# A wider row pitch for the two large tiles of the last layers, and message products taken by column

## The chip, the cores and the metric

The kernel runs on one core of a Trainium2 chip. The metric is the device time of one execution in microseconds. Five engines work side by side, each in the order of its own queue: PE (matrix products), DVE and ACT (elementwise work), POOL (elementwise work as well) and SP, which here only issues DMAs.

## What is computed

The input x is 4 images of 128 x 128 pixels with 128 channels. Four layers follow, each of the form x + f(group norm of x): a deformable convolution, a convolution that runs along the rows of the image as a recurrence, a message layer and a triangle product. The change concerns the last two; cut to what matters:

```python
# layer 2, messages: inputs = group norm of x, [b, m, k, d]
message_m = sum(inputs, axis=2)            # over k
message_k = sum(inputs, axis=1)            # over m
z = inputs @ Wself.T + (message_m @ Wm.T)[:, :, None] + (message_k @ Wk.T)[:, None]
x = x + z
# layer 3, triangle: xn = layer_norm(group norm of x)
left  = (xn @ left_w  + left_b)  * sigmoid(xn @ lgate_w + lgate_b)
right = (xn @ right_w + right_b) * sigmoid(xn @ rgate_w + rgate_b)
out   = einsum('bkjd,bkid->bijd', left, right)
out   = layer_norm(out) * sigmoid(xn @ ogate_w + ogate_b)
x = x + out @ to_out_w + to_out_b
```

## The kernel before

The first two layers, `deform_layer` and `scan_layer`, take the first 3,950 us or so and leave their result in device memory as x2T, channels first. `message_and_triangle` does the rest, one image after the other, in three parts.

`taken_in(b)` forms the tile X of one image: 128 channels on the partitions and, in each, 128 x 128 values of 4 bytes, with the image's column w (named j later on) ahead of its row h (named i), so that one column is a run of 512 B. Its first loop, the message loop, takes eight image rows at a time (16 iterations an image): SP loads them as x2c (L1274), POOL adds the two message terms into zc (L1276), PE multiplies x2c by the weights in two products of 512 columns each (L1282), and DVE adds product and zc into X (L1285). Because the product has its columns in the order (h, w) and X lies in the order (w, h), the store of L1285 steps by 512 B from element to element. Two `bn_stats` on DVE follow (L1290), which read X in runs of four elements. After the loop eight DMAs store X to device memory as x3T (L1295), to be added to the output later. The second loop takes 16 columns at a time: PE multiplies X by a centring matrix (L1316), ACT squares the result (L1322) and writes it back into X (L1325), the deviations go to device memory, are inverted and come back spread over all partitions as rwide (L1350), and DVE multiplies X by them (L1354).

`multiplied(b)` forms the tile T: PE multiplies X by the stacked weights (L1369), ACT takes the sigmoid (L1374), DVE multiplies the two and stores them into T by channel (L1375), each channel being a row of 128 values, 512 B; then products of two such rows (L1393) go back into T through ACT (L1397). The gate goes to device memory (L1382 to L1389).

`given_out(b, T)` goes through the result by column j. It reads `prod[:, :, j]`, 128 elements of one j, one from each row of T and so 512 B apart: once for the statistics (L1409, DVE, 16 at a time), once for the normalized u (three of four on ACT, L1438, the fourth on POOL, L1434). Then PE transposes u (L1451), ACT scales (L1453), POOL multiplies by the gate that was loaded (L1446, L1454), PE adds x3 and multiplies by the output weights (L1457, L1460), ACT copies to the gate's tile (L1461), and SP stores that (L1462).

The order of work: the queues are in the order of the program, up to small moves by the scheduler. While `given_out(b)` runs, every half step of it (four columns j) is followed by two steps of the generator `taken_in(b + 1)`, so the message loop of the next image lies beside the output of this one. The tile pools set how far things run ahead: zc and sq share one buffer (the tag in_work), x2c has two buffers, rwide two of its own, the gate two, X and T one each. All DMAs of this stage are issued from SP's queue.

Of the kernel before, what the change touches and what calls it, by code (L numbers as in the profile page):

```python
# [10 lines left out]
F32 = mybir.dt.float32  # L11
I32 = mybir.dt.int32
BF16 = mybir.dt.bfloat16
AF = mybir.ActivationFunctionType
ALU = mybir.AluOpType
# [4 lines left out]
P = 128  # L20
B = 4
S = 128
# [10 lines left out]
NQ = 4  # L33
DQ = P // NQ
# [1120 lines left out]
def message_and_triangle(tc, c, x2T, counted, w2, w3, out, x3T, gateT, stdT):  # L1155
# [4 lines left out]
    nc = tc.nc  # L1160
# [4 lines left out]
    JB = 8  # L1165
    with ExitStack() as ctx:
# [29 lines left out]
        with tc.tile_pool(name="l3prep", bufs=1) as prep, tc.tile_pool(  # L1196
            name="l3ps_w", bufs=2, space=PSUM
# [48 lines left out]
        xs = {}  # L1246

        def taken_in(b):

            X = xs[b] = big.tile([P, S, S], F32, name="X")  # L1250
# [21 lines left out]
            for y0 in range(0, S, JB):  # L1272
                x2c = two.tile([P, JB, S], F32, name="x2c")
                nc.sync.dma_start(x2c, x2T[b, :, y0 : y0 + JB, :])  # L1274
                zc = one.tile([P, JB, S], F32, name="zc", tag="in_work")
                nc.gpsimd.tensor_tensor(  # L1276
                    zc, z[:, 0, y0 : y0 + JB].unsqueeze(2).to_broadcast([P, JB, S]),
                    z[:, 1].unsqueeze(1).to_broadcast([P, JB, S]), ALU.add,
                )
                pz = pair()  # L1280
                for h in range(2):
                    nc.tensor.matmul(  # L1282
                        pz[:, h], lhsT=ws, rhs=x2c[:, 4 * h : 4 * h + 4], start=True, stop=True
                    )
                nc.vector.tensor_tensor(  # L1285
                    X[:, :, y0 : y0 + JB].rearrange("p w h -> p h w"),
                    pz.rearrange("p n (h w) -> p (n h) w", w=S), zc, ALU.add,
                )
                for h in range(0, JB, 4):
                    nc.vector.bn_stats(  # L1290
                        stats3[:, (y0 + h) // 4, :], X[:, :, y0 + h : y0 + h + 4]
                    )
                yield
# [16 lines left out]
            for j0 in range(0, S, 2 * JB):  # L1310
                pv = single()
                for h in range(2):
                    j1 = j0 + h * JB
                    px = pair()
                    for n in range(2):
# [10 lines left out]
                        X[:, j1 : j1 + JB, :].rearrange("p j i -> p (j i)"), flat, AF.Identity,  # L1326
                        bias=ct,
# [19 lines left out]
                for h in range(4):  # L1347
                    j1 = j0 + h * 4
                    rw = two.tile([P, 4 * S], F32, name="rwide")
# [3 lines left out]
                    flat = X[:, j1 : j1 + 4, :].rearrange("p j i -> p (j i)")  # L1353
                    nc.vector.tensor_tensor(flat, flat, rw, ALU.mult)  # L1354
# [4 lines left out]
        def multiplied(b):  # L1359
# [3 lines left out]
            T = big.tile([P, NQ + 1, DQ, S], F32, name="T")  # L1363
# [186 lines left out]
```

## Time and profile before

| What | us |
|---|---|
| Median of 3 runs | 5,704.68 (5,692.88 to 5,705.37) |
| The profiled execution, its own time | 5,716.77 |
| Span of the profile | 5,715.0 |
| PE busy | 5,055.9 (88%) |
| DVE busy | 3,207.3 (56%) |
| ACT busy | 2,556.8 (45%) |
| POOL busy | 1,162.6 (20%) |
| DMA, mean rate over the span | 124 GB/s |

The durations in this document come from the profiled execution, which is 12 us above the median. A share of busy time over the whole span says little here, because the stages have different limits; the prediction reads the stage that the change touches, stretch by stretch. Three kinds of lines occur. A group or source line gives an instruction of one kernel line, how often it ran and its minimum, median and maximum in ns. A timeline line gives start and length in us, and in brackets how long the engine had stood idle and what ended that. The chain of waits follows back from the last instruction what released each step. One instruction's duration includes a latency that the next one overlaps, so the distance between two starts in a train is shorter than the duration.

### The profile page before, as it was taken

The numbers are of one execution on the slowest core, as the hardware profiler recorded it, in microseconds if no ns is written. First come the engines' busy times: TensorE is split into PE (matmuls) and PEld (weight loads), VectorE is DVE, ScalarE is ACT, GpSimd is POOL, SyncE is SP. The second block draws the span as 40 slices with busy tenths as digits, with TensorE's granted clock in tenths as the row PEclk, the third lists the DMA queues.
The fourth block names the chain that finished last, engine by engine and source line by source line (L and its number), as shares of the span: only waits on it lengthen the run. The fifth ranks groups of instructions, "written<-read, shape, count | busy, mean of one in ns | idle before, by whom it ended". The sixth has DMA issues, their size and how long they took to land. (4 is left out here: it accounts for less than half of the span.)

```text
span 5715.0 us, 163429 instructions
## 1 busy us (share of the span) xinstructions
PE 5055.9 (88%) x69432; PEld 4359.9 (76%) x69432; DVE 3207.3 (56%) x8190; ACT 2556.8 (45%) x5243; POOL 1162.6 (20%) x1013
## 2 busy tenths in 40 slices
PE   2898999999999999899998999997797887887886
PEld 1787788787887888788997999996474774774775
DVE  4666666666666666655555666666446245345350
ACT  1554454544545445445442333331445445446444
POOL 4222222201212012221000111112104204214112
PEclk9999999999999999999998999999999999999987
DMA  4776566665666756556442222222417317327324
GB/s 150 155 166 148 128 148 133 154 132 114 148 135 144 142 103 146 130 125 130 87 92 79 78 87 77 77 87 75 149 49 238 129 66 235 118 79 230 111 70 134
DMA packets 1273820, 710.73 MB, mean 124 GB/s; under 512 B 845645, under 2 KB 1112174, under 8 KB 1263862
## 3 DMA queue, kind: packets, MB, share of 16 engines
q1 hardware_dynamic: 1243538, 658.56, 46.1%
q10 hardware_dynamic: 29540, 41.60, 2.1%
q8 instruction: 549, 8.99, 0.7%
q14 instruction: 193, 1.58, 0.1%
HBM read 417.28 MB, written 282.55 MB: 122 GB/s over the span
## 5 line engine op out<-in xcount | busy, mean ns | idle before, releaser
L606 PE MATMUL conv_ps<-ring,wdef 128*128 128x192 f32 (+2 forms) x7632 | 1295.4, 319 | 5.8 <-DVE x1c L576 4.8
L514 DVE TENSOR_TENSOR m<-t_ps,tent 128x390 f32<-128x390 f32 x1548 | 806.9, 557 | 785.1 <-ACT tent L512 769.2
L606 PEld LDWEIGHTS conv_ps<-ring,wdef 128*128 128x128 f32 x7632 | 1141.5, 194 | 125.3 <-issue 64.0
L512 ACT COPY tent<-t_ps 128x390 f32<-128x390 f32 x1560 | 691.4, 487 | 652.6 <-PE t_ps L498 642.4
L498 PE MATMUL t_ps<-parts_of,spread 57*64 57x99 bf16 (+1 forms) x12384 | 741.7, 275 | 167.2 <-DVE m L514 145.0
L523 PE MATMUL v_ps<-m,pixels 60*64 60x108 f32 (+1 forms) x22704 | 813.7, 265 | 18.4 <-DVE m L514 8.8
L498 PEld LDWEIGHTS <-spread 57*64 57x64 bf16 x12480 | 577.5, 125 | 311.8 <-issue 264.5
L523 PEld LDWEIGHTS v_ps<-m,pixels 60*64 60x64 f32 x22704 | 674.0, 137 | 68.7 <-DVE m L514 23.1
L549 ACT COPY ring<-v_ps 128x432 f32<-128x432 f32 x1032 | 505.7, 525 | 445.1 <-PE v_ps L523 444.4
L420 POOL TENSOR_TENSOR off<-off,koff 72x512 f32<-72x512 f32 x128 | 162.7, 1271 | 1761.8 <-DVE off L417 1761.8
L1369 PEld LDWEIGHTS pair_ps<-wcat,X 128*128 128x128 f32 x4096 | 474.3, 192 | 52.3 <-POOL X L1356 23.2
L1369 PE MATMUL pair_ps<-wcat,X 128*128 128x128 f32 x4096 | 495.9, 279 | 19.8 <-POOL X L1356 18.2
L1375 DVE TENSOR_TENSOR T<-pair_ps,sig 128x512 f32<-128x512 f32 x256 | 266.8, 1043 | 424.1 <-ACT sig L1374 415.5
L1110 PEld LDWEIGHTS own_ps<-diff,wconv 128*128 128x128 f32 x4064 | 494.4, 191 | 13.2
L1110 PE MATMUL own_ps<-diff,wconv 128*128 128x128 f32 x4064 | 495.2, 273 | 0.0
L506 PE MATMUL t_ps<-parts_of,spread 57*64 57x130 bf16 x9288 | 454.2, 225 | 0.0
L1150 POOL TENSOR_TENSOR sum_h<-sum_h,x2c 128x512 f32<-128x512 f32 x128 | 162.5, 1269 | 1137.9 <-DVE x2c L1136 680.4
L438 DVE SCALAR_TENSOR_TENSOR parts<-off,parts 72x512 bf16<-72x512 f32 x384 | 296.1, 772 | 150.7 <-ACT parts L430 145.0
L1460 PE MATMUL one_ps<-outw,y 128*128 128x128 f32 x1024 | 247.6, 334 | 122.5 <-POOL y L1454 122.4
L1068 ACT ACTIVATE rowT<-x1T_ps,t_x,s_x 128x128 f32<-128x128 f32 x512 | 207.7, 568 | 313.2 <-PE x1T_ps L1064 313.2
L1460 PEld LDWEIGHTS one_ps<-outw,y 128*128 128x128 f32 x1024 | 195.2, 239 | 174.5 <-POOL y L1454 172.7
L506 PEld LDWEIGHTS <-spread 57*64 57x64 bf16 x9312 | 318.8, 108 | 0.1
(183 smaller groups left out, 6930.0 us busy)
## 6 DMA issues: line engine op xcount, KB each, us to landing
pixels<-tab SPq DMA_DIRECT2D x688, 123.8 KB
parts_of<-off SPq DMA_DIRECT2D x1032, 55.7 KB
off<-parts SPq DMA_DIRECT2D x64, 891.0 KB
tab<-rows SPq DMA_DIRECT2D x384, 128.0 KB
xin<-in_x_dram SPq DMA_DIRECT2D x128, 256.0 KB
x<-x1c SPq DMA_DIRECT2D x32, 1024.0 KB
x1rows<-x SPq DMA_DIRECT2D x128, 256.0 KB
x2T<-x2c ACTq DMA_DIRECT2D x128, 256.0 KB
```

The source lines that it names most:

```text
L438: nc.vector.scalar_tensor_tensor(parts[:, NSPLIT + i, h : h + RO, 2 : S + 2], off, 0.0, part, ALU.is_gt, ALU.mult,)
L498: nc.tensor.matmul(tp[h : h + HALF, 0, 0:n].rearrange("p (r c) -> p r c", c=PADW)[:, :, i:PADW:RX], lhsT=spread[0:k, kx // 2, i, h : h + H ...
L506: nc.tensor.matmul(tp[h : h + HALF, 1, i * PADW : (i + 1) * PADW], lhsT=spread[HALF : HALF + k, kx // 2, first + i, h : h + HALF], rhs=src ...
L512: nc.scalar.copy(tent[:, 0:n], tp[:, 0, 0:n])
L514: nc.vector.tensor_tensor(m, *pair, ALU.mult)
L523: nc.tensor.matmul(to[p1 : p1 + HALF], lhsT=pix[p0 : p0 + LANES, xb, :], rhs=m[p0 : p0 + LANES, :, RX * xb : RX * xb + w], start=True, sto ...
L549: nc.scalar.copy(to, bodies[side])
L606: nc.tensor.matmul(pc[:, at : at + rows, x0:x1], lhsT=wdef[:, side, k, :], rhs=v[:, :, k if v.shape[2] == NK else kx, x0 + kx : x1 + kx], ...
L1110: nc.tensor.matmul(own[:, n], lhsT=wt[:, 2 * j + n, :], rhs=diffs[h][:, n, :, j : j + V], start=False, stop=(n == 1 and j == NJ - 1),)
L1369: nc.tensor.matmul(pj[:, j], lhsT=X[:, j0 + j, :], rhs=wcat[:, q * 4 * DQ : (q + 1) * 4 * DQ], start=True, stop=True,)
L1375: nc.vector.tensor_tensor(T[:, q : NQ + 1 : NQ - q, :, j0 : j0 + JB], pj[:, :, 0 : 2 * DQ].rearrange("p j (n d) -> p n d j", n=2), sig.rea ...
L1460: nc.tensor.matmul(po[:, j], lhsT=y[:, j], rhs=outw, start=False, stop=True)
```

## The change

Both large tiles get rows of 132 elements (528 B) of which 128 are used. The message loop forms its product by column: the moving operand of the two products reads x2c with the row h as the inner dimension (eight elements, 512 B apart, x2c itself keeps its layout), so the product has the order (w, h) of X; zc is formed in the same order, and the store into X is in runs of eight elements. To make room, rwide uses the buffers of x2c. The other edits only give the views of X and T a third dimension, since rows are no longer adjacent; the DMA into x3T keeps its line but now leaves X in rows of 128 elements.

```diff
+    PITCH = S + 4
...
-            X = xs[b] = big.tile([P, S, S], F32, name="X")
+            X = xs[b] = big.tile([P, S, PITCH], F32, name="X")[:, :, 0:S]
...
-                zc = one.tile([P, JB, S], F32, name="zc", tag="in_work")
+
+                zc = one.tile([P, S, JB], F32, name="zc", tag="in_work")
                 nc.gpsimd.tensor_tensor(
-                    zc, z[:, 0, y0 : y0 + JB].unsqueeze(2).to_broadcast([P, JB, S]),
-                    z[:, 1].unsqueeze(1).to_broadcast([P, JB, S]), ALU.add,
+                    zc, z[:, 0, y0 : y0 + JB].unsqueeze(1).to_broadcast([P, S, JB]),
+                    z[:, 1].unsqueeze(2).to_broadcast([P, S, JB]), ALU.add,
                 )
                 pz = pair()
                 for h in range(2):
+                    w = slice(h * S // 2, (h + 1) * S // 2)
                     nc.tensor.matmul(
-                        pz[:, h], lhsT=ws, rhs=x2c[:, 4 * h : 4 * h + 4], start=True, stop=True
+                        pz[:, h], lhsT=ws, rhs=x2c[:, :, w].rearrange("p h w -> p w h"),
+                        start=True, stop=True,
                     )
                 nc.vector.tensor_tensor(
-                    X[:, :, y0 : y0 + JB].rearrange("p w h -> p h w"),
-                    pz.rearrange("p n (h w) -> p (n h) w", w=S), zc, ALU.add,
+                    X[:, :, y0 : y0 + JB], pz.rearrange("p n (w h) -> p (n w) h", h=JB), zc,
+                    ALU.add,
                 )
...
                     nc.scalar.activation(
-                        X[:, j1 : j1 + JB, :].rearrange("p j i -> p (j i)"), flat, AF.Identity,
-                        bias=ct,
+                        X[:, j1 : j1 + JB, :], flat.rearrange("p (j i) -> p j i", i=S),
+                        AF.Identity, bias=ct,
                     )
...
-                    rw = two.tile([P, 4 * S], F32, name="rwide")
+                    rw = two.tile([P, 4 * S], F32, name="rwide", tag="x2c")
...
-                    flat = X[:, j1 : j1 + 4, :].rearrange("p j i -> p (j i)")
-                    nc.vector.tensor_tensor(flat, flat, rw, ALU.mult)
+                    nc.vector.tensor_tensor(
+                        X[:, j1 : j1 + 4, :], X[:, j1 : j1 + 4, :],
+                        rw.rearrange("p (j i) -> p j i", i=S), ALU.mult,
+                    )
...
-            T = big.tile([P, NQ + 1, DQ, S], F32, name="T")
+            T = big.tile([P, NQ + 1, DQ, PITCH], F32, name="T")[:, :, :, 0:S]
```

## The prediction

> **What bounds the kernel now.** The change touches only the last two layers, which start at about 3,950 us; everything before is left alone. I read the busy table by stretch of that stage first. Its columns are the stretch and its length, the busy time of PE, PE's weight loads, DVE, ACT and POOL (with counts), granted clock, DMA share, GB/s.
>
> ```profile
> 3950.00:4020.00 70.00, 35.56 (x70) 12.84 (x70) 55.02 (x65) 0.29 (x1) 30.32 (x16) 0.88 0.50 157
> 4704.00:4772.00 68.00, 51.12 (x229) 31.61 (x227) 61.85 (x101) 23.86 (x44) 44.76 (x32) 0.95 0.74 230
> 4772.00:4800.00 28.00, 22.80 (x96) 13.73 (x98) 16.17 (x67) 16.77 (x26) 5.96 (x7) 0.82 0.87 338
> ...
> 4520.00:4684.00 164.00, 162.65 (x1214) 142.89 (x1215) 59.59 (x58) 69.11 (x120) 0.00 (x0) 1.00 0.15 53
> 5516.00:5715.00 199.00, 120.20 (x646) 109.96 (x644) 50.40 (x176) 93.91 (x171) 58.11 (x64) 0.72 0.41 124
> ```
>
> The reader is to see four regimes. The message loop (rows 1 and 2: alone, and beside the previous image's output) is held by DVE: 55 of 70 and 62 of 68 us. Row 3, after that loop, is held by DMA (0.87 busy). The products with X and T (row 4) are held by PE, 162.65 of 164 us. The last image's output (row 5) has no full engine: there the chain of waits runs over the gate's load, multiplication and store.
>
> Then the timeline, to see what alternates (start, length, engine, line), and one line of the chain of waits:
>
> ```profile
> 3958.78 1.90 POOL L1276 TENSOR_TENSOR zc<-z 128x1024 f32<-128x1024 f32 x1 [2.02 <-DVE X L1285]
> ...
> 3960.71 1.88 DVE L1285 TENSOR_TENSOR X<-pair_ps,zc 128x1024 f32<-128x1024 f32 x1 [0.69 <-POOL zc L1276]
> ...
> 3962.67 1.90 POOL L1276 TENSOR_TENSOR zc<-z 128x1024 f32<-128x1024 f32 x1 [2.00 <-DVE X L1285]
> ...
> 4685.06 4.73 DVE L1409 BATCH_NORM_STATS2 st<-T 128x6 f32<-128x128 f32 x17 [13.48 <-ACT T L1397]
> ...
> 4770.23 8.20 SPq L1295 DMA_DIRECT2D x3T<-X  x8
> ```
>
> ```profile
> 4782.92 10.84 DMA out_dram<-gate
> ```
>
> POOL's zc and DVE's X share one buffer, so they take turns: 1.90 + 1.91 + hand-over = 3.9 us an iteration. Ahead of each image's output DVE runs a train of statistics st, one every 0.27 us. After the loop eight stores of 1 MB go out, and the next output store waits 10.84 us behind them.
>
> Last, the single instructions (minimum/median/maximum ns):
>
> ```profile
> L1285 DVE TENSOR_TENSOR X<-pair_ps,zc x64: 1870/1912/1949, 3952.9 to 5186.8; 128x1024 f32<-128x1024 f32 x64
> ...
> L1290 DVE BATCH_NORM_STATS2 stats<-X x128: 662/676/696, 3954.8 to 5189.4; 128x6 f32<-128x512 f32 x128
> ...
> L342 DVE BATCH_NORM_STATS2 stats<-xhalf x768: 198/209/219, 166.0 to 2048.9; 128x6 f32<-128x64 f32 x192
> ...
> L1409 DVE BATCH_NORM_STATS2 st<-T x512: 273/361/405, 4269.2 to 5558.0; 128x6 f32<-128x128 f32 x171
> ...
> L1354 DVE TENSOR_TENSOR X<-X,rwide x128: 628/693/1612, 4058.9 to 5322.8; 128x512 f32<-128x512 f32 x128
> ...
> L1136 DVE TENSOR_TENSOR x2c<-x1T_ps,carry x256: 414/422/429, 3085.2 to 3933.3; 128x256 f32<-128x256 f32 x128
> ```
>
> They price a step of 512 B. Statistics of 64 and of 512 elements in runs of four take 209 and 676 ns, a slope of 1.04 ns and so 276 ns for 128; L1409, which reads T one element per 512 B, takes 361: 85 ns too much. L1285 writes X one element per 512 B: from L1354's 693 ns for 512 elements, 1,024 should take 693 + 512 x 1.04 = 1,225; it takes 1,912, 687 ns too much. On ACT, a train of six L1438 (reads T at 512 B) lasts 3.09 us, a start every 0.50 us; a train of four L1068, also 128 elements with the same two per-partition operands but a contiguous read, lasts 1.63 us, every 0.355 us: 144 ns too much.
>
> **What the skill says.** "SBUF — State Buffer", in the note on cachelines under "Door 1: The DMA port swizzle", has lines of 16 bytes, and every access that crosses to a new line pays. That explains the excesses, but by it a pitch of 528 B helps nothing: each element still lies on a new line. The trace of before half agrees: L1290's runs of four are free. But L1136 reads alternately from two places 544 B apart and takes 422 ns, what its 256 elements cost by the slope (693 - 256 x 1.04 = 427). So steps that are no multiple of 512 B look free; I go with the trace. "GPSIMD Engine Reference", "Performance pitfalls for Q7 kernels", charges reads with a step over 8 bytes; 528 is over it too, so L1434's u on POOL keeps its 0.55 us. The same page, "Elementwise — side-by-side cycle accounting", has addresses generated in hardware and a loop bound that is the number of elements: zc with rows of 8 instead of 128 should keep 1.90 us. No run here shows such rows. "DMA: Bandwidth & Descriptors", "Specifications", asks for 512 B at least; the stores stay just there.
>
> **The change, part by part**, against the profiled execution (5,716.8 us, span 5,715.0; 12.1 us above the median 5,704.7 of three runs).
>
> 1. X written by column: runs of 8 elements, and contiguous reads. L1290's runs of four and L551's runs of two at a 520 B pitch (203 ns for 54 elements) show no excess, so 1,912 becomes 1,225 ns. Alone, an iteration goes from 3.9 to 3.2 us: 16 x 0.69 = -11 us. Beside the output, two iterations and one half step of output take 8.1 us now (4,705.6 to 4,770.2 over 8). After: zc, X, zc, X with hand-overs 2 x (1.90 + 1.22 + 0.07) = 6.4, and part of POOL's y and u (1.27 + 0.58) that does not fit into its waits, 0.4: 6.8. DVE needs 7.7 - 1.4 - 0.3 = 6.0, less than that. 8 x 1.27 = 10 us, three images: -30 us.
>
> 2. The product's moving operand read by column, one element per 512 B of x2c (x2c has no pitch). Not shown for PE. Floor: the present 0.43 us between L1282's starts; ceiling: twice ACT's excess per element (1.13 ns x 2 x 512 = 1.15) on top, 1.6 us. No gain is possible, since no contiguous read becomes faster by scattering. I take one ACT-like excess, 1.0 us. Alone that is 2.0 of 3.2 us. Beside the output, four of them with 12 short products at 0.11 us and four transposes are 5.8 of 6.8 us. Hidden by the zc/X alternation; cost nothing, at its ceiling it takes the loop's gain.
>
> 3. T at 528 B: st loses 85 ns. In the chain of waits of one image's output (4,684 to 4,940 us) st holds 6.3% or 16 us, 58 of them at 0.278: -4.7 us an image, three images, and about -3 in the last: -17 us. u on ACT loses 144 ns, but is on the chain only some 12 times an image: -2 us each, four images: -8 us; the rest (ACT 55 us busier now in all) is off the chain. L1375 keeps its 1,043 ns, because its other operands step by 256 and 512 B too; it lies under PE anyway (59.6 of 164 us).
>
> 4. The x3T stores leave X in pieces of 512 B instead of 8 KB. In the trace's packets the 8,192 B ones of this stage took 314 ns (median), those of 512 B 27 to 29. An image is 524,288 B an engine: 64 x 314 = 20 us against 1,024 x 28.8 = 29.5 us: +9 us. These stores are what stops the output store for 10.84 us, so I charge all of it: 3 x 9 = +27 us, and +7 for the first image, whose deviations queue behind them (bounds: 0 if they hide, 45 if the issues on SP lengthen too; behind them on SP stand the gate loads, x3 loads and output stores).
>
> 5. rwide moves into x2c's two buffers. Its loads wait for the last products, long done; the next image's first two x2c loads wait for the last rwide instead of being early, and stand ahead of gateT stores on SP. They are needed some 150 us later: nothing. Three-dimensional views of L1325, L1354 and L1356 keep runs of 128: nothing.
>
> Sum: -11 - 30 - 17 - 8 + 27 + 7 = -32 us: 5,716.8 becomes 5,685, and on the scale of the median **5,673**.
>
> **Rivals.** (a) *Everything pays*: the stores hide behind a shorter loop and only 5 us of item 4 stay, ACT's relief counts double: -41 - 17 - 16 + 5 = -69, 5,636. For it: the loop ends earlier, and DMA has slack before and after row 3. Against: row 3's 338 GB/s. (b) *The pitch does nothing*, the page is right and L1136 is special: only item 1 and item 4 remain, -41 + 34 = -7, 5,698. (c) *Slower: PE's column read.* Place: the message loop; price m per product. From m = 1.25 us PE takes over from zc/X; with the loop's time 16 x (2m - 3.9) + 24 x (4m + 1.8 - 8.1) and +9 from the rest, the gain is gone at 1.6 us, and at m = 1.9 it is about 5,744. For it: PE takes 429 ns for 512 contiguous columns and nothing bounds its scattered read. Against: DVE and ACT pay no more than 1.2 ns an element.
>
> **Chances.** A difference of 0.3% (17 us) is about what a measurement of this kernel can tell from none. Forecast 0.47, (a) 0.20, (b) 0.15, (c) 0.18. Faster: most of the forecast, (a), a little of (b): 0.64. Same: most of (b), edges of the others: 0.19. Slower: (c): 0.17. The range goes from (a) with a few us more, 5,632, over (b) to 5,722, and leaves most of (c) out.
>
> **What would show it.** L1285 near 1.23 us and zc still 1.90; st near 276 ns, L1438 about 0.36 us apart; L1282 between 0.8 and 1.1 us apart; packets of 512 B for x3T and a wait of the output store nearer 18 than 11 us after the loop; row 4 unchanged. I am wrong if zc grows past 2.5 us, if L1282 passes 1.25 us, or if st and u keep their times.

## The result and the profile after

| Kernel | Median (lowest to highest), us | Runs |
|---|---|---|
| before | 5,705.02 (5,692.88 to 5,707.67) | 4 |
| after | 5,757.29 (5,753.05 to 5,765.92) | 4 |

The change makes the kernel slower: the medians differ by 52 us, and the ratio of the times is 1.0100 with a 95% interval of 1.0083 to 1.0116. The forecast was 5,673 us, faster by 32. A second set of runs of the same two kernels gave 5,758.47 against 5,706.99 us, ratio 1.0081 [1.0063, 1.0098]. The profiled execution of after took 5,755.54 us, with a span of 5,753.8; that of before, as said, lay 12 us above its median.

The first view to read again is the busy time by stretch of the last two layers (stretch, length, then busy time of PE, its weight loads, DVE, ACT and POOL, granted clock, DMA share, GB/s). This is the kernel after; the rows stand in the order of those shown of before: the first message loop alone, a message loop beside an image's output, the stretch that follows it, the products with X and T, the last image's output.

```profile
3950.00:4012.00 62.00, 57.52 (x69) 12.71 (x67) 41.60 (x54) 0.00 (x0) 31.18 (x16) 0.96 0.38 121
4720.00:4793.00 73.00, 72.95 (x229) 31.06 (x228) 50.41 (x97) 23.07 (x41) 45.39 (x32) 0.99 0.59 187
4793.00:4825.00 32.00, 17.99 (x64) 9.24 (x64) 18.12 (x71) 16.86 (x26) 3.47 (x5) 0.81 0.99 286
4536.00:4699.00 163.00, 162.12 (x1211) 142.34 (x1212) 59.58 (x57) 68.47 (x120) 0.00 (x0) 1.00 0.14 53
5556.00:5754.00 198.00, 118.88 (x650) 108.81 (x648) 51.08 (x176) 95.03 (x171) 58.18 (x64) 0.75 0.40 125
```

Rows 4 and 5 are as before: 162.12 of 163 us on PE, and an output of 198 us. The loss is in rows 2 and 3. In row 2 DVE did what was forecast, 50.41 instead of 61.85 us, and it bought nothing, for PE is now busy 72.95 of 73 us: the loop has a new bound, and is longer. In row 3 the DMA engines are busy 0.99 of the time at 286 GB/s, where before they were 0.87 busy at 338.

The single instructions of the kernel after say why (minimum, median and maximum in ns, first and last start in us):

```profile
L1278 POOL TENSOR_TENSOR zc<-z x64: 1944/1948/1961, 3951.4 to 5217.3; 128x1024 f32<-128x1024 f32 x64
...
L1285 PE MATMUL pair_ps<-x2c,ws x256: 1022/1040/1112, 3950.9 to 5217.8; 128*128 128x512 f32 x128
L1289 DVE TENSOR_TENSOR X<-pair_ps,zc x64: 1223/1224/1226, 3954.7 to 5219.2; 128x1024 f32<-128x1024 f32 x64
...
L1415 DVE BATCH_NORM_STATS2 st<-T x512: 279/374/441, 4266.1 to 5599.7; 128x6 f32<-128x128 f32 x171
...
L1444 ACT ACTIVATE u<-T,nm,rs x384: 592/607/654, 4275.3 to 5720.6; 128x128 f32<-128x128 f32 x192
```

The store into X (L1289) takes 1,224 ns, forecast 1,225; zc (L1278) takes 1,948, where the prediction had kept it at 1,900. The statistics st (L1415) take 374 ns and u (L1444) 607: with rows 528 B apart both are a little slower than before (361 and 596), not faster. And the message product is in the profile 256 times. The source has 4 images × 16 iterations × 2 halves = 128 products, so one fp32 product is two PE instructions. The line of the same product of before, which the prediction had read only for the distance between starts, has the same count:

```profile
L1282 PE MATMUL pair_ps<-x2c,ws x256: 592/592/1219, 3950.5 to 5183.8; 128*128 128x512 f32 x128
```

The starts of these instructions in a train stood 429 ns apart before and stand 863 ns apart after; an iteration has four of them, not two. The chain of waits of the kernel after, over 4,718 to 4,793 us, is in its shares by engine and line:

```profile
by line: PE pair_ps L1285 73.7%; PE one_ps L1466 10.7%; PE one_ps L1463 10.1%; PE one_ps L1457 4.7%; PE one_ps L1264 0.5%; PE one_ps L1266 0.3%; PE one_ps L1265 0.3%; issue 0.1%; ACTq L1467 0.0%
```

Nothing but PE is left on the chain: 73.7% are the message products, and the rest are the short products and transposes of the output (L1457, L1463, L1466), which wait in line with them. The timeline of the kernel after shows the hand-over in the loop that runs alone (start, length, engine, line; in brackets the idle time and what ended it):

```profile
3954.40 11.88 PE L1285 MATMUL pair_ps<-x2c,ws 128*128 128x512 f32 x13
3954.68 1.23 DVE L1289 TENSOR_TENSOR X<-pair_ps,zc 128x1024 f32<-128x1024 f32 x1 [3.41 <-PE pair_ps L1285]
3955.99 1.95 POOL L1278 TENSOR_TENSOR zc<-z 128x1024 f32<-128x1024 f32 x1 [2.69 <-DVE X L1289]
3958.13 1.23 DVE L1289 TENSOR_TENSOR X<-pair_ps,zc 128x1024 f32<-128x1024 f32 x1 [0.91 <-PE pair_ps L1285]
```

PE runs without a gap in this stretch, and DVE's store is released by PE, no longer by POOL's zc. The stores start 3.45 us apart: four times 0.863.

The other loss is in SP's queue after a loop (kernel after):

```profile
4793.65 2.70 SPq L1468 DMA_DIRECT2D out_dram<-gate  x1
4796.40 22.15 SPq L1299 DMA_DIRECT2D x3T<-X  x7
4818.65 4.31 SPq L1468 DMA_DIRECT2D out_dram<-gate  x1
4823.00 0.75 SPq L1452 DMA_DIRECT2D gate<-gateT  x1
```

Before, all eight x3T stores were issued within 8.20 us. Now seven of them hold SP for 22.15 us, and what stands behind them in the queue, an output store and a gate load, is issued that much later. In the packet records the stores were 1,024 packets of 8,192 B, median 314 ns, and are 16,384 packets of 512 B, median 27 ns. From the first packet of an image to its last, the 8.39 MB took 20.5 to 21.2 us in the first three images before (395 to 409 GB/s; 23.4 us in the last), and take 29.6 to 30.1 us now (279 to 283 GB/s); over the middle half of the packets alone the rates are 416 to 422 and 286 to 288 GB/s.

For the experiments I use three measures of a profile. The *loop* of an image is from the start of its first store into X to the start of its last, 15 of the 16 steps from store to store. The *drain* is from there to the start of the first multiplication by rwide (L1354 of before), the stretch in which the x3T stores leave. The third is a product's start-to-start distance in a train.

| us | loops, images 0 to 3 | drains, images 0 to 3 |
|---|---|---|
| before | 58.3, 60.7, 60.8, 60.7 | 47.7, 37.4, 36.3, 38.1 |
| after | 54.6, 67.5, 67.6, 67.6 | 46.7, 47.6, 47.3, 47.2 |

The first loop is 3.7 shorter, the other three together 20.5 longer, the last three drains together 30.3 longer and the first 1.0 shorter: +46 us, against 52 between the medians. In further profiles of the same two kernels each loop repeats within 0.2 us and each drain within 1.5; in three other kernels that leave the loop as it was, one of the four loops takes 1.4 to 1.6 us longer. Whole stages don't repeat as well: the time from the first store into X to the end was 1,762.2 and 1,745.0 us in two profiles of before, 1,799.1 and 1,795.9 in two of after, and the unchanged layers ahead end up to 27 us apart. So a difference of a few us is read from loops and drains, and of whole kernels only the ratios count. A ratio in this document is the one on record with its interval; it isn't the quotient of the two medians beside it, and differs from that by up to 0.001.

### The profile page after: what moved, and what is told of

Same layout as the page of the kernel before. It is cut to its first block, busy times and chain, and to the rows that moved or that the text cites. A ratio compares the mean times of both kernels' runs of the same rounds, so it can differ in the third digit from the quotient of the medians.

```text
span 5753.8 us, 163432 instructions
## 1 busy us (share of the span) xinstructions
PE 5139.9 (89%) x69432; PEld 4360.2 (76%) x69432; DVE 3171.8 (55%) x8190; ACT 2556.6 (44%) x5243; POOL 1164.9 (20%) x1013
## 5 line engine op out<-in xcount | busy, mean ns | idle before, releaser
L1375 PE MATMUL pair_ps<-wcat,X 128*128 128x128 f32 x4096 | 500.7, 280 | 21.1 <-POOL X L1362 14.6
L1375 PEld LDWEIGHTS pair_ps<-wcat,X 128*128 128x128 f32 x4096 | 478.0, 194 | 54.7 <-DVE T L1381 23.2
L1381 DVE TENSOR_TENSOR T<-pair_ps,sig 128x512 f32<-128x512 f32 x256 | 266.8, 1043 | 423.7 <-ACT sig L1380 415.5
L1466 PE MATMUL one_ps<-outw,y 128*128 128x128 f32 x1024 | 243.1, 330 | 109.3 <-POOL y L1460 109.3
L1466 PEld LDWEIGHTS one_ps<-outw,y 128*128 128x128 f32 x1024 | 197.5, 239 | 170.0 <-POOL y L1460 153.3
```

Source lines behind the costliest of these rows:

```text
L1375: nc.tensor.matmul(pj[:, j], lhsT=X[:, j0 + j, :], rhs=wcat[:, q * 4 * DQ : (q + 1) * 4 * DQ], start=True, stop=True,)
L1381: nc.vector.tensor_tensor(T[:, q : NQ + 1 : NQ - q, :, j0 : j0 + JB], pj[:, :, 0 : 2 * DQ].rearrange("p j (n d) -> p n d j", n=2), sig.rea ...
L1466: nc.tensor.matmul(po[:, j], lhsT=y[:, j], rhs=outw, start=False, stop=True)
```

## Experiments

Each ran beside the kernel before on the same chip; ratios are to that. The letters of the theories mean what the text of each expectation gives them. A line that begins with L is from the view of single instructions: minimum, median and maximum in ns, first and last start in us.

### The columns without the pitch

The kernel after with both pitches taken out and rwide in its own buffers, so that of the change the message loop by column remains:

```diff
-    PITCH = S + 4
+    PITCH = S
...
-                    rw = two.tile([P, 4 * S], F32, name="rwide", tag="x2c")
+                    rw = two.tile([P, 4 * S], F32, name="rwide")
```

> The column products without any pitch: X, T and rwide's buffers as before, x3T leaves X in 8 KB pieces. Theory A (two causes: PE's column read costs about 7 us in each message loop that runs beside an output and gains 3.5 us in the first one; the finer x3T pieces cost about 10 us an image): only the first cause is left, -3.5 + 3 x 7 = +17 us, 5,722 us; product starts 0.86 us apart, the stretch from the end of the message loop to the first rwide multiplication back at 37 us. Theory B (the shared buffers of x2c and rwide, or the pitch itself, make the loss): nothing is left of it, 5,700 us or less, since the store into X still falls to 1.22 us.

Measured: 5,738.0 us against 5,720.21, ratio 1.0031 [1.0017, 1.0045]. Loops 57.3, 67.4, 67.5 and 67.6, drains 47.0, 39.9, 39.5 and 36.7 us, starts 863 ns apart. The product's line in this kernel:

```profile
L1285 PE MATMUL pair_ps<-x2c,ws x256: 1022/1040/1113, 3954.4 to 5208.4; 128*128 128x512 f32 x128
```

The line is that of after to a nanosecond: the doubled product belongs to the column read of x2c, and the pitches have no part in it. The three later loops are 6.7 to 6.9 us longer than before. The first is only 1.0 shorter, where 3.5 were expected; why is open. The drains are nearly back at those of before, so the longer drain belongs to the pitch or to the shared buffers, which a run below rules out.

### The pitch without the columns

The kernel after with zc, the products and the store into X as they were before:

```diff
-                        pz[:, h], lhsT=ws, rhs=x2c[:, :, w].rearrange("p h w -> p w h"),
-                        start=True, stop=True,
+                        pz[:, h], lhsT=ws, rhs=x2c[:, 4 * h : 4 * h + 4], start=True, stop=True
...
-                    X[:, :, y0 : y0 + JB], pz.rearrange("p n (w h) -> p (n w) h", h=JB), zc,
-                    ALU.add,
+                    X[:, :, y0 : y0 + JB].rearrange("p w h -> p h w"),
+                    pz.rearrange("p n (h w) -> p (n h) w", w=S), zc, ALU.add,
```

> The pitch of X and T and the shared buffers, with the products and the store in the order of before. Theory A: the message loop is as before (61 us) if 528 B is no better for the store than 512 B (1.91 us), and the x3T pieces cost 10 us in three images and up to 9 in the first: 5,735 to 5,745 us. Theory C (528 B does free the scattered store, as the prediction took for reads): the store falls to 1.23 us, message loops 10 us shorter, 5,700 us. Theory B (shared buffers): also above before, but with the delay ahead of the message loop and not behind it.

Measured: 5,761.42 against 5,720.21 us, ratio 1.0079 [1.0052, 1.0106]. Loops 59.6, 61.7, 61.7 and 61.7, drains 47.2, 46.5, 46.7 and 47.2 us; st 370 ns, u 607. The store into X in this kernel:

```profile
L1287 DVE TENSOR_TENSOR X<-pair_ps,zc x64: 1954/1996/2037, 3970.5 to 5220.4; 128x1024 f32<-128x1024 f32 x64
```

The pitch alone is a loss. The store into X still puts each element 528 B from the one before, and takes 1,996 ns instead of 1,912: this step, no multiple of 512 B, saves nothing. The drains are those of after.

### The moving operand at a pitch too

The kernel after with the pitch moved from T to x2c, so that PE's column read goes in steps of 528 B:

```diff
-                x2c = two.tile([P, JB, S], F32, name="x2c")
+                x2c = two.tile([P, JB, PITCH], F32, name="x2c")[:, :, 0:S]
...
-            T = big.tile([P, NQ + 1, DQ, PITCH], F32, name="T")[:, :, :, 0:S]
+            T = big.tile([P, NQ + 1, DQ, S], F32, name="T")
```

> The changed kernel with x2c's rows at 528 B as well, so PE's column read steps by 528 B, and T without a pitch (for room). Theory A1 (a scattered read costs PE the same at any step over a few bytes): product starts stay 0.86 us apart, 5,757 us, perhaps some us more since x2c then arrives in 512 B pieces. Theory A2 (only steps that are multiples of 512 B cost): starts fall to 0.43 us, the loop to 52 us beside an output and 3.2 us an iteration alone, 5,757 - 4 - 3 x 14 = 5,711 us. T without its pitch: st and u 11 to 13 ns shorter, about -3 us.

Measured: 5,777.54 against 5,720.21 us, ratio 1.0102 [1.0075, 1.0129]. Starts 893 ns apart, loops 60.7, 69.2, 69.2 and 69.2 us. The product's line in this kernel:

```profile
L1285 PE MATMUL pair_ps<-x2c,ws x256: 1049/1074/1215, 3970.3 to 5247.7; 128*128 128x512 f32 x128
```

PE doesn't gain from a pitched operand either; its instruction becomes 34 ns longer (1,074 against 1,040). And st (361 ns) and u (597) went back to their old times with T's old rows.

### T at a pitch that is no multiple of 16 B

The kernel before, T alone in rows of 516 B:

```diff
-            T = big.tile([P, NQ + 1, DQ, S], F32, name="T")
+            T = big.tile([P, NQ + 1, DQ, S + 1], F32, name="T")[:, :, :, 0:S]
```

> The kernel before with one edit: T's rows at 516 B instead of 512 B. If scattered reads cost the same at every step (theory A): st stays at 361 to 375 ns, u at 596 to 607, 5,705 us. If only certain steps are slow and 528 B was the wrong one: st falls to 276 ns, u to about 455, 5,680 us.

Measured: 5,717.68 against 5,720.21 us, ratio 1.0003 [0.9990, 1.0015]. The two readers of T in this kernel:

```profile
L1409 DVE BATCH_NORM_STATS2 st<-T x512: 285/372/432, 4268.7 to 5556.3; 128x6 f32<-128x128 f32 x171
...
L1438 ACT ACTIVATE u<-T,nm,rs x384: 594/607/653, 4278.0 to 5679.0; 128x128 f32<-128x128 f32 x192
```

Another pitch, the same 372 and 607 ns. T's pitch is worth nothing in either direction within the interval, and the value 528 was not at fault.

### Steps of 4 B to 640 B

What a step costs, measured by itself: in the kernel before, after the first image's T is complete, trains of four instructions of each kind over 96 elements, at sixteen steps. "Alternating" reads or writes by turns at two places 544 B apart, as L1136 does, whose price the prediction had built on. These trains are added work; what they write is not read or is written over later.

```diff
+            for s in (1, 2, 3, 4, 8, 16, 32, 64, 128, 129, 130, 132, 136, 144, 160, 0):
+                for k in range(4):
+                    nc.scalar.activation(
+                        flat(to, s), stepped(t, s), AF.Identity, bias=obcol, scale=ogcol
+                    )
...
+                    nc.tensor.matmul(
+                        flat(po, s), lhsT=outw, rhs=stepped(t, s), start=True, stop=True
+                    )
...
+                    nc.vector.tensor_tensor(
+                        stepped(x, s), flat(wcat[:, 0:NE], s), flat(wcat[:, NE : 2 * NE], s),
+                        ALU.add,
+                    )
```

> The kernel before with trains of four equal instructions put behind the first image's T: 96 elements read or written at steps of 1, 2, 3, 4, 8, 16, 32, 64, 128, 129, 130, 132, 136, 144 and 160 elements, and alternately from two places 136 elements apart (as L1136 does): an ACT read (two per-partition operands), a DVE statistic, a PE moving read, a DVE two-operand read and a DVE two-operand store. X is overwritten afterwards, so nothing of the output changes. Theory A (a price for every element that lies on another 16-byte line than the last): the price is there from step 4 on and the same at 64, 128, 132 and 160; alternating between two places is free or half price. Theory A2 (multiples of 512 B): only 128 pays. For PE, from the changed kernel: 0.85 ns an element from the same step on.

Measured (a single run, 5,736.19 us), ns for 96 elements. For PE it is the distance between the starts of instructions, of which a product has two, as the count below shows (64 products in the source); for the others the duration of one.

| Step in elements (B) | PE reads | ACT reads | DVE reads, statistics | DVE stores |
|---|---|---|---|---|
| 1 (4) | 112 | 468 | 260 | 258 |
| 2 (8) | 112 | 472 | 261 | 260 |
| 3 (12) | 130 | 516 | 292 | 292 |
| 4 (16) | 173 | 558 | 352 | 338 |
| 8 (32) | 174 | 560 | 334 | 320 |
| 128 (512) | 167 | 558 | 332 | 325 |
| 132 (528) | 173 | 568 | 335 | 330 |
| 160 (640) | 167 | 540 | 326 | 329 |
| alternating | 112 | 480 | 247 (one addition) | 330 |

In the order of the columns, the steps left out (16, 32, 64, 129, 130, 136 and 144 elements) lie at 164 to 183, 545 to 590, 316 to 341 and 305 to 340 ns. The alternating DVE read is a two-operand addition, because the statistics had no such train: 247 ns is the shortest of four, of which the others took 493 to 1,444, and contiguous ones took 243 to 269.

PE's 112 ns is a floor: at 429 ns for 512 columns, 96 contiguous ones would take 80, so steps that cost up to 32 ns don't show on PE. The count of PE's instructions in this kernel, from the view of single instructions:

```profile
L1387 PE MATMUL one_ps<-T,outw x128: 248/343/365, 4285.9 to 4305.9; 128*128 128x96 f32 x128
```

On three engines the price sets in within 16 B and then stays: about half of it at 12 B, all at 16 B, the same at 128 and 132 elements. That is what the Trainium skill states in "SBUF — State Buffer", in the cacheline note under "Door 1: The DMA port swizzle": lines of 16 bytes, two accesses to a line needed for full rate, each crossing to a new line paid. Steps of 8 B, two elements to a line, are free here. The last row shows where the prediction had gone astray: alternating *reads* are free or nearly so although they jump 544 B (on PE as far as its floor lets one see, on DVE by the one addition above and by L1136 itself), alternating *stores* are not. L1136 was cheap because of the order of its reads, not because 544 is no multiple of 512: read in steps of 516, 520 or 528 B, without coming back to a line, the same tile costs at least as much as at 512.

### The turn in the read of the accumulators

If PE must not read by column, something else can turn the product: DVE's own read of PSUM. The kernel before with zc in the order (w, h) and contiguous runs into X, the products left alone:

```diff
-                zc = one.tile([P, JB, S], F32, name="zc", tag="in_work")
+                zc = one.tile([P, S, JB], F32, name="zc", tag="in_work")
...
-                    X[:, :, y0 : y0 + JB].rearrange("p w h -> p h w"),
-                    pz.rearrange("p n (h w) -> p (n h) w", w=S), zc, ALU.add,
+                    X[:, :, y0 : y0 + JB],
+                    pz.rearrange("p n (h w) -> p w (n h)", w=S), zc, ALU.add,
```

> The kernel before, with the turn from rows to columns put into DVE's read of the product (512 B steps in PSUM) instead of its store; PE reads x2c contiguously, X has no pitch, zc is in column order. Theory A (every operand that steps costs about 0.7 ns an element on DVE, whichever side it is on): X takes 1.9 us again and the time is that of before, within 0.3%. Theory D (only a scattered store or a scattered SBUF read costs): X falls to 1.22 us, products stay 0.43 us apart, and the message loops get what the prediction wanted: 52 us beside an output, about -35 us.

Measured: 5,679.68 against 5,719.58 us, ratio 0.9934 [0.9912, 0.9956], some 38 us faster than before. Loops 49.3, 55.0, 54.0 and 53.7, drains 46.2, 36.9, 36.8 and 37.5 us. The busy time of the loop alone and of the loop beside an output, of this kernel, in the columns of the first table of busy times:

```profile
3946.00:3998.00 52.00, 29.97 (x62) 10.24 (x60) 39.28 (x47) 0.00 (x0) 30.26 (x16) 0.99 0.56 162
4684.00:4740.00 56.00, 46.18 (x213) 27.72 (x211) 48.28 (x87) 22.55 (x41) 43.88 (x32) 1.00 0.80 251
```

The product and the store in the same kernel:

```profile
L1282 PE MATMUL pair_ps<-x2c,ws x256: 592/592/1061, 3944.6 to 5142.8; 128*128 128x512 f32 x128
...
L1285 DVE TENSOR_TENSOR X<-pair_ps,zc x64: 1199/1225/1226, 3947.1 to 5146.2; 128x1024 f32<-128x1024 f32 x64
```

DVE reads PSUM in steps of 512 B at the price of a contiguous read: 1,225 ns for 1,024 elements, what it takes in after, where it reads PSUM in order. It gets the change's gain (item 1 of the prediction) without PE's loss, and is the fastest of all kernels here. No engine is full in its loop beside the output (48.28 of 56 us on DVE, 46.18 on PE).

### The same with the pitch

The kernel after with that loop: the change as it is, except that the turn is in DVE's read and not in PE's.

```diff
-                        pz[:, h], lhsT=ws, rhs=x2c[:, :, w].rearrange("p h w -> p w h"),
-                        start=True, stop=True,
+                        pz[:, h], lhsT=ws, rhs=x2c[:, 4 * h : 4 * h + 4], start=True, stop=True
...
-                    X[:, :, y0 : y0 + JB], pz.rearrange("p n (w h) -> p (n w) h", h=JB), zc,
-                    ALU.add,
+                    X[:, :, y0 : y0 + JB],
+                    pz.rearrange("p n (h w) -> p w (n h)", w=S), zc, ALU.add,
```

> The changed kernel with one part undone: PE reads x2c contiguously again, and DVE turns rows into columns in its read of the product in PSUM, as in the run that was faster than before; pitch and shared buffers stay. Theory A (the two losses add up): the gain of that run, -38 us, and the pitch's loss, +24 to +45 us, meet: within 0.3% of before. If the pitch's loss hides once the message loop is shorter: -30 us or more.

Measured: 5,709.78 against 5,708.75 us, ratio 1.0004 [0.9994, 1.0014]. Loops 49.2, 53.6, 53.6 and 53.6, drains 46.4, 46.5, 47.2 and 47.3 us. The store into X in this kernel:

```profile
L1287 DVE TENSOR_TENSOR X<-pair_ps,zc x64: 1198/1224/1227, 3955.6 to 5169.0; 128x1024 f32<-128x1024 f32 x64
```

The loops are as short as without a pitch, and the drains as long as in after: the rest of the change eats the whole gain, (1.0004 / 0.9934 - 1) x 5,705 = 40 us. Against this kernel the change differs only in who turns the product: its ratio of 1.0100, or 1.0081 in the second set, over 1.0004 puts PE's column read at 44 to 55 us; the loops alone give 47.

### Blocks of four rows

Another way to contiguous runs: the recurrence keeps and stores x2c as (w, four rows), so that the product comes out in that order with no strided read on PE.

```diff
-                x2c = two.tile([P, B, RB, S], F32, name="x2c")
+                xb = two.tile([P, B, S, RB], F32, name="x2c")
+                x2c = xb.rearrange("p b w r -> p b r w")
...
-                    X[:, :, y0 : y0 + JB].rearrange("p w h -> p h w"),
-                    pz.rearrange("p n (h w) -> p (n h) w", w=S), zc, ALU.add,
+                    X[:, :, y0 : y0 + JB].rearrange("p w (n r) -> p n w r", r=4),
+                    pz.rearrange("p n (w r) -> p n w r", r=4), zc, ALU.add,
```

> The kernel before, with the recurrence's output x2c kept and stored in blocks of four rows, (w, 4 rows), so that the products of the message loop read it contiguously and yet come out by column, and the store into X is in runs of four; no pitch, x3T in 8 KB pieces. The scatter moves to the recurrence: two stores of 256 elements a row there step by 16 B, the sum over w and the sum on POOL read with that step. Theory A: store 1.22 us, products 0.43 us apart, message loop 3.3 us an iteration alone and 52 to 55 us beside an output: -10 - 3 x 8 = -34 us in the last layers; in the recurrence DVE has 2 x 0.17 us a row and 1.4 us every four rows more, 128 rows: 0 to +88 us, depending on how much of it DVE's waits for PE take up (it waits 251 us there), so about +20: -15 us in all. If the 16 B step costs nothing: -34 us.

Measured: 5,724.71 against 5,719.58 us, ratio 1.0015 [1.0004, 1.0026], where 15 us less were expected. Loops 48.5, 52.9, 53.7 and 55.0 us, as short as with the turn in PSUM. But the last layers' first store starts at 4,001.9 us instead of 3,952.9 (3,947 to 3,974 in the other kernels). In the groups of the recurrence (3,080 to 3,940 us of this kernel; after the bar the busy time in us, the mean of one in ns and the idle time):

```profile
L1137 DVE TENSOR_TENSOR x2c<-x1T_ps,carry 128x256 f32<-128x256 f32 x244 | 150.9, 618 | 0.0
...
L1152 DVE TENSOR_REDUCE sum_w<-x2c 128x16 f32<-128x2048 f32 x30 | 115.6, 3854 | 0.0
```

The store of a row took 422 ns before and takes 618 with steps of 16 B; the sum over w took 2,269 and takes 3,854. Of 256 stores and 32 sums that makes 256 x 0.196 + 32 x 1.585 = 101 us of DVE, of which some 28 to 55 show in that later start. The gain was given back where the stride had been moved to.

### The pieces without the pitch

The kernel before, the x3T stores cut differently: every eighth row in one store, so that pieces of 512 B leave an unpitched X.

```diff
-            for j0 in range(0, S, 16):
-                nc.sync.dma_start(x3T[b, :, j0 : j0 + 16, :], X[:, j0 : j0 + 16, :])
+            for j0 in range(8):
+                nc.sync.dma_start(x3T[b, :, j0:S:8, :], X[:, j0:S:8, :])
```

> The kernel before with one edit: each of the eight x3T stores takes every eighth column of X instead of sixteen adjacent ones, so the same bytes leave in pieces of 512 B, without any pitch and without shared buffers. Theory A (DMA engines drain 512 B pieces at 290 instead of 420 GB/s and everything behind them waits): the stretch from the end of the message loop to the first rwide multiplication grows from 37 to 47 us in images 1 to 3, little in image 0, +25 to +30 us. Theory B (the loss of the pitch kernel comes from the pitch itself or from the shared buffers): same time as before.

Measured: 5,723.4 against 5,708.75 us, ratio 1.0028 [1.0017, 1.0038], so +16 [10, 22] us, where 25 to 30 were expected. Loops as before but for one (62.1), drains 41.2, 45.6, 44.9 and 46.4 us. SP's queue after a loop of this kernel:

```profile
4787.91 24.67 SPq L1295 DMA_DIRECT2D x3T<-X  x8
4812.68 3.50 SPq L1462 DMA_DIRECT2D out_dram<-gate  x1
```

Small pieces alone lengthen the issue as in after, and the drain by about 8 us in each of the last three images; the first drain is 6.5 shorter. These pieces also land scattered in device memory, where those of after land in order; no run separates the two.

### X alone at 516 B

The kernel before with the pitch on X only, 516 B, in the row order of before:

```diff
+    PITCH = S + 1
...
-            X = xs[b] = big.tile([P, S, S], F32, name="X")
+            X = xs[b] = big.tile([P, S, PITCH], F32, name="X")[:, :, 0:S]
```

> The kernel before with X's rows at 516 B and nothing else (rows order, T without pitch, rwide in its own buffers); x3T leaves in 512 B pieces because X's rows are no longer adjacent. Theory A: the whole of the pitch's cost is here, +25 to +45 us, drains of 46 us in images 1 to 3. Theory B (the sharing costs): +12 to +20 us, as with the pieces alone.

Measured: 5,754.61 against 5,719.67 us, ratio 1.0058 [1.0039, 1.0077], +33 [22, 44] us. Loops 59.9, 61.7, 61.8 and 61.7, drains 48.4, 47.0, 46.5 and 48.6 us. SP's queue after a loop of this kernel:

```profile
4794.48 24.35 SPq L1297 DMA_DIRECT2D x3T<-X  x8
```

The store, again from the view of single instructions of this kernel:

```profile
L1287 DVE TENSOR_TENSOR X<-pair_ps,zc x64: 1971/1999/2084, 3959.8 to 5216.5; 128x1024 f32<-128x1024 f32 x64
```

So the pitch's cost is X's: eight stores hold SP for 24.35 us, the three drains are 30 us longer together, and the strided store into X gains nothing from 516 B either (1,999 ns).

### rwide in x2c's buffers

The kernel before with only this line of the change:

```diff
-                    rw = two.tile([P, 4 * S], F32, name="rwide")
+                    rw = two.tile([P, 4 * S], F32, name="rwide", tag="x2c")
```

> The kernel before with one edit: rwide takes the two buffers of x2c. The pitch as a whole cost 39 to 45 us in two comparisons, finer x3T pieces without a pitch 16 us. Theory A (the rest of the pitch's cost is in X's layout and the pieces): 0, within 0.15% of before. Theory B (part of it is the sharing: the first loads of each new image wait for the last rwide and then stand ahead of other DMAs on SP): +15 to +25 us, to be seen ahead of the message loop or in the rwide phase.

Measured: 5,723.17 against 5,719.67 us, ratio 0.9996 [0.9983, 1.0009]. Sharing the buffers costs nothing that can be measured, at most 5 us by the interval, as the prediction had it.

### Both kernels again

> The changed kernel once more, with a second profile and more rounds. If the stage repeats: 1,797 to 1,803 us from the first store into X to the end, message loops beside an output 67.5 us, drains 47 us; the ratio of medians then comes nearer to 38 of 5,705 us, 1.007. If the loss is really 52 us, the ratio stays at 1.009 or more.

> The kernel before once more, for a second profile. In the first nine profiles the last layers alone (from the first store into X to the end) took 1,762 us before, 1,800 with the change, 1,781 with the columns alone, 1,787 with the pitch alone, while the first two layers, the same in all of these, ended anywhere from 3,947 to 3,974 us. If the last layers repeat to a few us (1,758 to 1,765), the stage's own length is the finer measure of the parts, and the medians' larger loss (52 us against 38) is scatter of the first layers. If they scatter by 10 us, no split finer than the medians' holds.

Measured: the change 5,758.47 against 5,706.99 us, ratio 1.0081 [1.0063, 1.0098], which lies between the two values expected and doesn't decide between them; before again, in a single run, 5,703.48 us. What the two profiles add is the repeatability given above: loops of 54.7, 67.4, 67.6 and 67.6 us in the one and 58.3, 60.7, 60.7 and 60.8 in the other.

## Why the prediction was wrong

It forecast a faster kernel, and the kernel became slower: 5,673 forecast, 5,757 measured, outside the range of 5,632 to 5,722. In order of its steps (two figures in a cell are, in steps 1 and 2, the first loop and the other three together; in step 3, the statistics and u; in step 4, the last three images and the first):

| Step | Forecast, us | Measured, us | From |
|---|---|---|---|
| 1. X stored in runs of eight | -11 - 30 | -9.1 - 21.4 | loops with the turn in PSUM and the pitch |
| 2. PE's column read | 0 | +5.4 + 41.9 | loops of after less those |
| 3. T at 528 B | -17 - 8 | within -6 and +9 | T at 516 B, ratio |
| 4. x3T stores in pieces | +27 + 7 | +30.3 - 1.0 | drains |
| 5. Shared buffers | 0 | within -10 and +5 | ratio |
| Sum | -32 | +46 from 1, 2 and 4; +52 by the medians | |

**Step 2 is the one that made the kernel slower:** without it the change is even with before (1.0004). It priced the product's column read at 1.0 us with a ceiling of 1.6 and called it hidden below 1.25. The time from start to start is indeed 0.86 us, inside the band that was written down for "L1282's starts" to show, but that is one *instruction*, and a product is two. The prediction took 429 ns for the whole product and put two in an iteration where there are four. With the count of 256 read against the source's 128, the same excess would have said 2 x 0.43 = 0.86 us for the product before, and the price asked of the step would have been twice its 1.0 us, over the point of 1.25 that it names itself. Rival (c), with its place and mechanism, is what happened: m is 2 x 0.863 = 1.73 us. Four instructions make 3.45 us an iteration, which is what the timeline shows in the loop alone. In the loop beside the output, two iterations take 8 x 0.863 + 1.8 = 8.7 us by the prediction's own term for the other products, against 8.1 before. That term was short as well: it has 12 short products, where the trace of after has 16 such instructions, 0.112 us apart, and four transposes at 0.109. Together 6.90 + 1.79 + 0.44 = 9.13 us, all of it on PE, and one train of four message instructions follows the next at that distance in the chain of waits (kernel after):

```profile
4742.27 3.46 PE pair_ps L1285 x4
4751.40 3.46 PE pair_ps L1285 x4
```

Rival (c) was given 0.18. Its formula with m = 1.73 gives -7 + 15 + 9 = +17 us, since it still counted T's gain of 25; without that +42.

**Step 1 held in its duration and less in its worth.** The store's 1,224 ns was forecast to within a nanosecond. Freed of PE's column read (in the kernel with the turn in PSUM and the pitch), a store follows the last after 3.28 us instead of 3.88 in the loop alone, and two follow in 7.17 instead of 8.10 beside an output: 16 x 0.60 = 9.6 us and 8 x 0.93 = 7.4 us an image, for 11 and 10 forecast (the table's figures cover 15 of the 16 steps). zc in rows of eight takes 1,948 ns and not 1,895, 16 x 0.053 = 0.8 us an image (in the rows of four of another run it took 1,896, so short rows as such are not what costs). What is left beside the output, some 0.2 us for two iterations, may lie in the 0.4 us that were estimated there for y and u; no run takes it apart.

**Step 3 failed altogether**, and with it 25 us of the gain. Reads of T at 528 B cost 11 to 13 ns more than at 512, and none of the 85 and 144 ns went away. The prediction had the page that says so before it, and set it aside for one line of the trace, L1136. The table of steps shows why that line misled: its reads alternate, and reads that alternate between two places 544 B apart are free or nearly so. It was evidence on an order of access, taken as evidence on a step. Rival (b), which rested on the page, was right in this. That L1375 keeps its 1,043 ns was right (1,045 in after). The reason given named operands in steps of 256 and of 512 B; since DVE's PSUM reads at 512 B turned out free, the one that pays should be the sigmoid's tile in SBUF, but no run took it alone.

**Step 4 held for the pitched kernel.** The sum of packets gave +9 us an image, and the drains of the last three images grew by 10.2, 11.0 and 9.1. The first image's, for which +7 had been charged, did not grow (-1.0). What the step put as a wait of the output store, "nearer 18 than 11 us", shows in another place: seven issues of L1299 hold SP's queue for 22.15 us, ahead of the output store and the gate load. "DMA: Bandwidth & Descriptors", "Specifications", asks for pieces of 512 B at least for line rate; the stores stayed at 512 B, and ran at 279 to 283 instead of 395 to 409 GB/s. So 512 B did not give here the rate that pieces of 8 KB reach; the measurement decides.

**Still open.** Small pieces alone cost 16 [10, 22] us and X's pitch 33 [22, 44]. X's pitch has the same pieces and a slower store into X, which is worth 1.6 us in the first loop and 1.0 in each of the others, 4.6 in all. Their drains are as long within 2.5 us in the last three images, and in the first 48.4 against 41.2, though the phase that follows (the multiplications by rwide) was 7 us longer in the kernel with the pieces alone. What remains between the two, some 12 us by the middle values, has a place: from the start of the drain to the last store into T (L1375 of before), images 1 to 3 take on average 313.7 to 318.0 us in the profiles whose X has no pitch and leaves in pieces of 8 KB, 319.9 with the pieces alone, and 323.7 to 326.2 in all those whose X has a pitch. With the pieces alone, the later phases make up part of the longer drain; with a pitch they don't. Why is not explained. The pitch without the columns (+45 [30, 60]) has loops and drains that add up to some 32; the stage's own scatter of 17 us can cover the rest, and no run decides it.

## What to carry to other kernels

Before pricing a product, divide the instructions of its line in the profile by the products in the source: a price per instruction is not a price per product, and here the factor of two made the loss: at 0.86 us a product would have stayed below the 1.25 us at which PE takes over. The cost of a strided operand doesn't vanish by being handed to another engine, only where the reader takes the stride for nothing; here that was DVE's read of PSUM (-38 us), not PE's read of SBUF, not a pitch, and not the store of an earlier layer. A pitch also cuts every transfer of the tile into rows, so price its DMAs along with its reads.

## What the runs showed of the hardware that was not expected

- An fp32 product of 128x128 by 512 columns is two PE instructions, each 429 ns from start to start on contiguous columns and 863 ns when each element lies 512 B from the last: (863 - 429) / 512 = 0.85 ns an element and instruction.
- Reads by PE, ACT and DVE and stores by DVE in SBUF pay for a step of 12 B (about half) and from 16 B on (all): (558 - 468) / 96 = 0.94 ns an element on ACT, (332 - 260) / 96 = 0.75 on DVE. Of the steps tried between 16 and 640 B none escapes it. Steps of 8 B are free, and reads that alternate between two places 544 B apart nearly so (480 ns against 468 on ACT); alternating stores are not (330 against 258 on DVE).
- DVE reads PSUM in steps of 512 B at no extra cost (1,225 ns for 1,024 elements, 1,224 in order).
- DMA pieces of 512 B take 27 ns on an engine, 8,192 B take 314: 279 to 283 GB/s against 395 to 409 over a store of 8.39 MB. From the fourth of eight stores on, each of 2,048 such pieces holds SP's queue for about 3.6 us (2.9 to 5.1 in the profile of after), against 1.25 for 128 pieces of 8,192 B.
